# GATv2 layer of 1,250 nodes: the norm between the two layers folded into the next matrices, tile ends issued in steps

## The chip, the core and the metric

The kernel runs on one core of a Trainium2 chip. The core has TensorE (PE, matrix products out of SBUF into PSUM; its weight loads are shown as PEld), VectorE (DVE), ScalarE (ACT), GpSimd (POOL) and SyncE (SP). Each has its own in-order queue, and they meet at semaphores. Data move between HBM and SBUF by DMAs that an engine issues. The metric is the device time of one execution in microseconds (us); lower is better.

## The reference

The inputs are 1,250 nodes with 768 features, 20,000 random edges (sorted by destination), and for each edge one of 34 types. All is float32. Two residual blocks follow one another:

```python
h = relu(layernorm(x))
x = x + gat(h)          # block 1, this case's subject
h = relu(layernorm(x))
x = x + rgcn_gcn(h)     # block 2: 34 relations, then one GCN, on 625-node halves of the indices
```

Block 1 is two GATv2 layers and two norms:

```python
def gatv2(x, Ws, bs, Wd, bd, attn):          # attn: H x D
    fs, fd = x @ Ws + bs, x @ Wd + bd        # N x H x D
    e = leaky_relu(fs[src] + fd[dst], 0.2)
    alpha = segment_softmax(einsum("ehd,hd->eh", e, attn), dst)
    return elu(segment_sum(alpha * fs[src], dst))

h1  = gatv2(h, W1s, b1s, W1d, b1d, attn1)    # 8 heads of 96
h2  = layer_norm(h1 + h) * ln1_w + ln1_b
out = gatv2(h2, Wos, bos, Wod, bod, attno)   # 1 head of 768
out = layer_norm(out) * lno_w + lno_b
```

`ln1_w` and `ln1_b` act per feature, and `h2` is only used as the left operand of the products with `Wos` and `Wod`. A node without an edge gets 0 from the segment sum.

## The kernel before

The kernel is written in a framework that places instructions on engines as the code says, but orders each engine's queue by its own scheduler, from the order of the code and the tiles' dependencies; pools with a number of buffers limit how far ahead a queue runs.

**Front end (0 to 177 us).** `fast_front` ranks the nodes by their number of incoming edges, highest first, by comparing them on TensorE and VectorE; rank and edge slots are scattered to a table in DRAM by GpSimd and read back as `rk` (L949, issued by SyncE), from which `perm`, `permg` and `degf` are copied. The first norm gives `h0` (written to DRAM by SyncE, L791), and its product with `W1s` the source table `fs_d` (L840; here a bias is added by a one-row product of a row of ones with the bias). SyncE also writes zeros and fill values to tables in DRAM (L809 to L815).

**Layer one (177 to 913 us).** The ranked nodes are cut into 10 tiles of 128, one node per partition. Tile k has as many edge slots as its largest degree, `CAPS = (33, 22, 20, 18, 17, 16, 15, 14, 13, 11)`, 179 in all; a tile of more than 20 slots is taken in two chunks, so there are 12 chunks. `attention` (L1189) works through them:

- `start_tile` (L1201) makes a tile's destination rows. In layer one `negated1` (L1407) gathers the tile's `h0` rows, transposes them by TensorE (`to_columns`, L1118; one or both copies out of PSUM by ScalarE, L1125, or the second by VectorE, L1127), multiplies them by `f_w1d` (`dense`, L1131: two halves of 384 columns, six matmuls each) and evicts the negative with the bias to `nfd` (L1414, VectorE).
- `front` (L1213) takes one slot: GpSimd gathers 128 rows of the source table into `fs`, a ring of 24 buffers; VectorE takes z = max(fs, nfd) (L1228), z times attn (L1233) and the sum per head (L1234), the slot's logits. `list_edges(row, n)` (L1388) lets GpSimd send n of the 179 pair scatters that build a later stage's list of edges (`r_pair_d`): 30 at slot 23 of tile 0, then 0.85 per slot, and more at the end.
- `softmax` (L1238) does the exponentials of a chunk; the sums of the two chunks of a tile are brought to one maximum.
- `back` (L1270) scales the slot's row by its weights (ScalarE, 8 instructions, L1286) and adds it into PSUM by a product with the identity, two halves (`ag`, L1288). `back` of a chunk runs beside `front` of the next one.
- `end` (L1302) divides by the softmax's sum (`share`, L1291), applies ELU and calls `finish1` (L1418): add `h0`, norm statistics and scaling (L1423), times `lnw` (L1424), plus `lnb` (L1425), transposes, product with `wos`, plus bias (`fs`, L1431), a product with a quarter of `attn_o` whose row sum is layer two's linear logit term (`wt`, L1433), scatter to the table `fs2_d` by GpSimd, product with `wod`, negative with bias (`fd`, L1440), and a write to DRAM (L1442).

The end of a tile is written whole after its last `back`, and the next-but-one tile's `start_tile` whole in the middle of a chunk. `loads1` (L1399) loads `wos`, `wod` and five rows broadcast to 128 partitions.

**Layer two (913 to 1,395 us)** is `attention` again with one head, `negated2` and `finish2` (L1467). Then come the relations (1,390 to 2,566 us), bound by TensorE, and the GCN.

Of the kernel before, what the change touches and what calls it, by code (L numbers as in the profile page):

```python
# [18 lines left out]
P = 128  # L19
# [607 lines left out]
def fast_front(ctx, tc, f, x, src, dst, edge_type, W1s, b1s, W1d, b1d, attn1, attno, W_rel):  # L627
# [26 lines left out]
    f.consts = ExitStack()  # L654
# [29 lines left out]
    with ExitStack() as front:  # L684
# [33 lines left out]
        ones_row = early.tile([1, P], F32, name="ones_row")  # L718
        nc.vector.memset(ones_row, 1.0)

        def by_heads(a, name):
            n, d = a.shape
            t = const.tile([P, n, d + 1], F32, name=name)
            nc.vector.memset(t[:, :, d], 1.0)
            nc.scalar.dma_start(t[:, :, :d], bass.AP(tensor=a.tensor, offset=a.offset, ap=[[0, P], [d, n], [1, d]]))
            return t

        f.attn_1 = by_heads(attn1, "attn_1")
        f.bias_1 = const.tile([P, D], F32, name="bias_1")
        nc.scalar.dma_start(f.bias_1, bass.AP(tensor=b1d.tensor, offset=b1d.offset, ap=[[0, P], [1, D]]))  # L730
        f.attn_o = by_heads(attno, "attn_o")


# [52 lines left out]
        for j in range(NT):  # L786
            n = min(P, N - j * P)
            row = xs[j]
            sc, sh = norm_scale(nc, small, f, row, n)
            nc.scalar.activation(row[:n], row[:n], AF.Relu, bias=sh[:n], scale=sc[:n])  # L790
            nc.sync.dma_start(f.h0_d[j * P:j * P + n, :], row[:n])  # L791
            to_columns(nc, ps_t, f, hT, j, row, n, both=True)
# [16 lines left out]
        nc.sync.dma_start(f.pair_d.rearrange("(p c) f -> p c f", p=P), fill)  # L809
        zero = prep.tile([P, D], F32, name="zero")  # L810
        nc.vector.memset(zero, 0.0)
        nc.sync.dma_start(f.h2_d[NP:, :], zero)
        for t in range(PT + 1):
            nc.sync.dma_start(f.h1_d[NP + t * P:NP + (t + 1) * P, :], zero)
        nc.sync.dma_start(f.h1_d[f.ZERO:, :], zero[:1])  # L815
# [133 lines left out]
        nc.sync.dma_start(rk, rank_d.rearrange("(k p) f -> p k f", p=P))  # L949
# [195 lines left out]
def fast_rest(ctx, tc, f, x, src, dst, edge_type, W1s, b1s, W1d, b1d, attn1, ln1_w, ln1_b,  # L1145
# [43 lines left out]
    def attention(H, table, negated, attn_e, first, loads, finish, rate, rest, give_back=lambda: None):  # L1189
# [12 lines left out]
        def start_tile(k):  # L1202
            t = Tile()
            t.k, t.S, t.done = k, CAPS[k], []
            t.nfd = rows_tile("nfd", 2)
            nc.vector.memset(t.nfd[:, :, HD], -BIG)
            negated(k, t.nfd[:, :, :HD])
            t.lg = None
            return t

        def front(c, i):

            t, s = c.t, c.first + i  # L1213
            fs = pool.tile([P, RW], F32, name="fs", tag="fs", bufs=ring)
            row = gather(fs[:, :W], table[:, :], f.rec[:, t.k, s, 0:1])
            fs = fs[:, :W].rearrange("p (h e) -> p h e", h=H)
            if t.k == 0 and s == ring - 1:
                list_edges(row, 30)
            elif t.k or s >= ring:
                list_edges(row, rate)  # L1220
            if t.k == NT - 1 and s == t.S - 1:
                list_edges(row, rest)
                f.last_row = row
            if t.lg is None:
                lg = pool.tile([P, S0 * f.H], F32, name="lg", tag="lg", bufs=2)
                t.lg = lg[:, :S0 * H].rearrange("p (s h) -> p s h", h=H)
            z = rows_tile("z", 2)
            nc.vector.tensor_tensor(z, fs, t.nfd, op=ALU.max)  # L1228
            if H == 1:
                nc.vector.scalar_tensor_tensor(z[:, 0, :], z[:, 0, :], 1.0, attn_e[:, 0, :], op0=ALU.mult,  # L1230
                                               op1=ALU.mult, accum_out=t.lg[:, s, :])
            else:
                nc.vector.tensor_mul(z, z, attn_e)  # L1233
                nc.vector.tensor_reduce(t.lg[:, s, :], z, axis=AX.X, op=ALU.add)  # L1234
            c.rows.append(fs)
# [55 lines left out]
        def share(o, ps, by):  # L1291

            if H == 1:
# [8 lines left out]
        def end(t):  # L1302
# [4 lines left out]
            share(o, c.ps, c.den)  # L1307
# [6 lines left out]
            finish(t.k, o)  # L1314
# [9 lines left out]
        tiles = {}  # L1324
# [10 lines left out]
        begin(0)  # L1335
        for i in range(chunks[0].n):
            front(chunks[0], i)
            if i == 3:
                loads()
            if i == chunks[0].n // 2:  # L1340
                begin(1)
        softmax(chunks[0])
        for j, now in enumerate(chunks):
            after = chunks[j + 1] if j + 1 < len(chunks) else None
            for i in range(max(now.n, after.n if after else 0)):
                if i < now.n and after:
                    back(now, i)
                if after and i < after.n:
                    front(after, i)
                if i == now.n // 2:  # L1350
                    begin(j + 2)
            if after:
                softmax(after)
                if j + 2 == len(chunks):
                    for i in range(after.n):
                        back(after, i)
                    give_back()
            if now.first + now.n == now.t.S:
                end(now.t)
# [6 lines left out]
                            f.degf[:, :, None].to_broadcast([P, NT, S0]), op=ALU.is_ge)  # L1366

# [27 lines left out]
    with ExitStack() as one:  # L1395
        bias_1 = f.bias_1
        late = {}

        def loads1():  # L1399
            ap1 = late["pool"] = one.enter_context(tc.tile_pool(name="r_att1", bufs=1, side="right"))  # L1400
            late["wos"], late["wod"] = load_w(ap1, Wos, "wos", "wos"), load_w(ap1, Wod, "wod", "wod")
            for name, a in (("lnw", ln1_w), ("lnb", ln1_b), ("bias_s", bos), ("bias_d", bod), ("attn_o", attno)):
                late[name] = load_row(ap1, a, name)
# [3 lines left out]
        def negated1(k, nfd):  # L1407
# [4 lines left out]
            to_columns(nc, ps_t, f, hT, 0, h0s[k], P, both=True)  # L1412
            ps = dense(nc, ps_t, f, hT, f.w1d, 0, P, tag="mm2")
            nc.vector.scalar_tensor_tensor(  # L1414
                nfd.rearrange("p (a h) d -> p a h d", a=2), ps[:, :, :HW].rearrange("p a (h d) -> p a h d", d=D // H),
                -1.0, bias_1.rearrange("p (a h d) -> p a h d", a=2, d=D // H), op0=ALU.mult, op1=ALU.subtract)

        def finish1(k, o):  # L1418
            lnw, lnb, wos, wod = late["lnw"], late["lnb"], late["wos"], late["wod"]
            bias_s, bias_d, attn_o = late["bias_s"], late["bias_d"], late["attn_o"]  # L1420
# [3 lines left out]
            nc.vector.tensor_mul(o, o, lnw)  # L1424
            nc.vector.tensor_add(o, o, lnb)  # L1425
            hT = pool.tile([P, KC, P], F32, name="hT1", tag="hT1", bufs=1)
            to_columns(nc, ps_t, f, hT, 0, o, P)
            ps = dense(nc, ps_t, f, hT, wos, 0, P, tag="mm2")
            ap1 = late["pool"]
            fs = ap1.tile([P, W2], F32, name="fs2", tag="fs2", bufs=1)  # L1430
            nc.vector.tensor_add(halves(fs, P, f), ps[:, :, :HW], halves(bias_s, P, f))  # L1431
            wt = work.tile([P, D], F32, name="wt2", tag="att_e")
            nc.vector.scalar_tensor_tensor(wt, fs[:, :D], SLOPE / (1.0 - SLOPE), attn_o, op0=ALU.mult, op1=ALU.mult,  # L1433
                                           accum_out=fs[:, D:])
            row = scatter(fs2_d[:, :], fs, f.perm[:, k:k + 1], "fs2")
            if NT - 4 < k < NT - 1:
                list_edges(row, 7 if k < NT - 2 else 40)
            ps = dense(nc, ps_t, f, hT, wod, 0, P, tag="mm2")
            fd = ap1.tile([P, D], F32, name="fd2", tag="fd2", bufs=1)
            nc.vector.scalar_tensor_tensor(halves(fd, P, f), ps[:, :, :HW], -1.0, halves(bias_d, P, f),  # L1440
                                           op0=ALU.mult, op1=ALU.subtract)
            nc.sync.dma_start(nfd2_d[k * P:(k + 1) * P, :], fd)  # L1442

        attention(H, f.fs_d, negated1, f.attn_1, prepare_lists, loads1, finish1, 0.85, 4)


# [11 lines left out]
    def loads2():  # L1458
        for name, a in (("lnw", lno_w), ("lnb", lno_b), ("bias_g", b_gcn)):
            late[name] = load_row(ap2, a, name)  # L1460
        late["ones"] = ap2.tile([1, P], F32, name="ones_r")
        nc.vector.memset(late["ones"], 1.0)
# [4 lines left out]
    def finish2(k, o):  # L1467
        lnw, lnb, bias_g = late["lnw"], late["lnb"], late["bias_g"]
        sc, sh = norm_scale(nc, small, f, o, P)
        row = ap2.tile([P, D], F32, name="x1", tag="x1", bufs=2)  # L1470
# [18 lines left out]
        def root():  # L1489
            ps, _ = dense(nc, ps_t, f, hT, late["wroot"], 0, P, tag="mm2", bias=(late["ones"], late["bias_r"]))  # L1490
# [5 lines left out]
        if k < NT - 3:  # L1496
            root()
        else:
            roots[k] = root

    def negated2(k, nfd):
        nc.sync.dma_start(nfd[:, 0, :], nfd2_d[k * P:(k + 1) * P, :])

    def read_lists():
# [9 lines left out]
        fold = rl.tile([P, P], F32, name="fold")  # L1514
# [10 lines left out]
    attention(1, fs2_d, negated2, f.attn_o, lambda: None, loads2, finish2, 0, 0, give_back)  # L1525
# [129 lines left out]


# [110 lines left out]
```

## Time and profile before

| | |
|---|---|
| time, median of 3 runs | 2768.38 us (2763.95 to 2773.92) |
| the profiled execution | 2772.99 us, span 2771.2 us |
| clock granted to TensorE, mean | 0.93 |
| PE / DVE / POOL / ACT busy | 2355.7 / 1560.9 / 1549.0 / 852.4 us |
| layer one: scalings L1286 on ScalarE | 370.0 us in 1,376 instructions |
| layer one: `ag` products L1288 on PE | 286.9 us in 716 records |
| layer one: L1228, L1233, L1234 on DVE | 169.8, 168.5, 168.0 us |
| layer one: `f_w1d`, `wos`, `wod` products on PE | 83.7, 82.4, 79.3 us, 240 records each |

The rows come from one profiled execution. Busy times are sums over the span, and each stage has another engine ahead, so they are to be read by stretches of time. A group of instructions is named by its line, engine, operation and the tiles it writes and reads; "idle before" is the engine's idle time just ahead of the group, with what ended it. One float32 matmul of the code appears as two records, so 240 records are 120 matmuls.

### The profile page before, as it was taken

How to read it: one execution, taken by the hardware profiler on the slowest of the kernel's cores; microseconds unless marked ns; L12 is line 12 of the kernel's file. 1: busy time of each engine (PE TensorE's matmuls, PEld its weight loads, DVE VectorE, ACT ScalarE, POOL GpSimd, SP SyncE). 2: the span in 40 equal slices, each digit the busy share in tenths (PEclk: the TensorE clock that was granted, in tenths of full speed). 3: DMA queues.
4: the chain of work that ended last, by engine and by line, in shares of the span. 5: the costliest groups of instructions: out<-in, count | busy, mean ns of one | idle time of the engine just before them, and what ended most of it. 6: DMA issues, size and time to landing. Idle time of an engine off the chain costs nothing. (4 is left out here: it accounts for less than half of the span.)

```text
span 2771.2 us, 24164 instructions
## 1 busy us (share of the span) xinstructions
PE 2355.7 (85%) x7759; PEld 1365.4 (49%) x7759; DVE 1560.9 (56%) x2360; ACT 852.4 (31%) x2308; POOL 1549.0 (56%) x1113
## 2 busy tenths in 40 slices
PE   3874484889998467889899999999999999999687
PEld 2431142445545234444456666666666666666254
DVE  7659779999996799999563222222232222210262
ACT  3003592778773122333312112211221212212010
POOL 3137787777872675778375544444444454431471
PEclk7986797999999788999999999999999999999899
DMA  7134453444540775677477777777777777766783
GB/s 248 41 128 146 115 147 95 127 129 131 154 123 29 246 234 170 202 214 216 160 241 194 200 189 187 189 197 197 192 194 187 185 191 197 174 165 152 217 264 117
DMA packets 136419, 476.82 MB, mean 172 GB/s; under 512 B 26323, under 2 KB 28396, under 8 KB 136285
## 3 DMA queue, kind: packets, MB, share of 16 engines
q0 software_dynamic: 83872, 334.60, 46.4%
q1 hardware_dynamic: 47755, 134.03, 13.6%
q10 hardware_dynamic: 4658, 6.57, 0.7%
q8 instruction: 64, 1.05, 0.1%
q14 instruction: 70, 0.57, 0.1%
HBM read 385.90 MB, written 89.32 MB: 171 GB/s over the span
## 5 line engine op out<-in xcount | busy, mean ns | idle before, releaser
L1135 PE MATMUL ps<-wrel,mT 128*128 128x384 f32 x3336 | 1099.1, 486 | 1.1 <-DMA wrel<-in_L_gnn_W_rel_dram 1.1
L1135 PEld LDWEIGHTS ps<-wrel,mT 128*128 128x128 f32 x3336 | 623.0, 190 | 407.1 <-DMA wrel<-in_L_gnn_W_rel_dram 1.0
L1164 POOL DMA_INDIRECT g<-r_h_d,lists x241 | 341.9, 1419 | 516.9 <-DVE g L1565 290.7
L1288 PE MATMUL ag<-fs,identf 128*128 128x384 f32 x716 | 286.9, 532 | 152.4 <-ACT fs L1286 142.0
L1565 DVE TENSOR_TENSOR g<-g,g 128x768 f32<-128x768 f32 x68 | 64.6, 950 | 612.5 <-DMA g<-r_h_d,lists 512.6
L1228 DVE TENSOR_TENSOR z<-fs,nfd 128x776 f32<-128x776 f32 (+1 forms) x358 | 348.5, 990 | 60.0 <-DMA fs<-f_fs_d,rec 37.2
L1286 ACT ACTIVATE fs<-fs,lg 128x96 f32<-128x96 f32 x1376 | 370.0, 363 | 0.3
L1278 PE MATMUL ag<-fs,dg 128*128 128x384 f32 x716 | 251.7, 512 | 81.0 <-ACT dg L1276 81.0
L1168 POOL DMA_INDIRECT r_pair_d<-rec,place x179 | 259.5, 1450 | 59.9 <-issue 46.7
L1164 POOL DMA_INDIRECT fs<-r_fs_d,rec x179 | 244.0, 1363 | 80.7 <-issue 33.4
L1592 POOL DMA_INDIRECT r_h_d<-y,lists x139 | 223.9, 1611 | 110.2 <-ACT y L1591 52.3
L1164 POOL DMA_INDIRECT fs<-f_fs_d,rec x179 | 236.7, 1323 | 77.0 <-issue 50.2
L1288 PEld LDWEIGHTS ag<-fs,identf 128*128 128x128 f32 x716 | 132.4, 200 | 294.0 <-ACT fs L1286 236.5
L1278 PEld LDWEIGHTS ag<-fs,dg 128*128 128x128 f32 x716 | 141.3, 200 | 188.0 <-ACT dg L1276 88.1
L1591 ACT ACTIVATE y<-ps,lists 128x768 f32<-128x768 f32 x71 | 64.0, 901 | 479.8 <-PE ps L1135 479.8
L1591 ACT ACTIVATE y<-ps,rcnt 128x768 f32<-128x768 f32 x68 | 61.3, 901 | 454.6 <-PE ps L1135 454.6
L1230 DVE SCALAR_TENSOR_TENSOR z<-z,attn_o 128x769 f32<-128x769 f32 x179 | 174.4, 993 | 0.0
L1697 DVE TENSOR_TENSOR acc<-acc,nb 128x768 f32<-128x768 f32 x69 | 66.2, 959 | 187.1 <-DMA nb<-r_h_d,srcz 186.3
L1233 DVE TENSOR_TENSOR z<-z,attn 128x776 f32<-128x776 f32 x179 | 168.5, 955 | 0.1
L1234 DVE TENSOR_REDUCE lg<-z 128x8 f32<-128x776 f32 x179 | 168.0, 950 | 0.1
L1627 DVE SCALAR_TENSOR_TENSOR arow<-node,from_f,arow 128x1250 f16<-128x1250 f16 x110 | 166.2, 1511 | 1.7
L1123 PEld LDWEIGHTS pt<-identf,g 128*128 128x128 f32 x834 | 99.8, 141 | 47.5 <-issue 24.5
(282 smaller groups left out, 2322.0 us busy)
## 6 DMA issues: line engine op xcount, KB each, us to landing
wrel<-in_L_gnn_W_rel_dram SPq DMA_DIRECT2D x37, 2304.0 KB
g<-r_h_d,lists POOLq DMA_INDIRECT x241, 4.8
r_nfd_d<-fd SPq DMA_DIRECT2D x10, 384.0 KB
nfd<-r_nfd_d SPq DMA_DIRECT2D x10, 384.0 KB
r_x_d<-xb SPq DMA_DIRECT2D x10, 384.0 KB
x1r<-r_x_d SPq DMA_DIRECT2D x10, 384.0 KB
f_fs_d<-o_s SPq DMA_DIRECT2D x9, 388.0 KB
x<-in_x_dram SPq DMA_DIRECT2D x9, 384.0 KB
```

Source lines behind the costliest of these rows:

```text
L1135: last = nc.tensor.matmul(ps[:n, half, :f.HW], hT[:, k, j * P:j * P + n], w[:, k, cols], start=(k == 0), stop=(k == f.KC - 1 and not bias))
L1164: return nc.gpsimd.indirect_dma_start(out=to, out_offset=None, in_=table, in_offset=bass.IndirectOffsetOnAxis(ap=idx, axis=0))
L1168: s = nc.gpsimd.indirect_dma_start(out=table, out_offset=bass.IndirectOffsetOnAxis(ap=idx, axis=0), in_=rows, in_offset=None, **kw)
L1228: nc.vector.tensor_tensor(z, fs, t.nfd, op=ALU.max)
L1230: nc.vector.scalar_tensor_tensor(z[:, 0, :], z[:, 0, :], 1.0, attn_e[:, 0, :], op0=ALU.mult, op1=ALU.mult, accum_out=t.lg[:, s, :])
L1233: nc.vector.tensor_mul(z, z, attn_e)
L1234: nc.vector.tensor_reduce(t.lg[:, s, :], z, axis=AX.X, op=ALU.add)
L1278: nc.tensor.matmul(c.ps[:, half, :HW], dg, fs[:, 0, half * HW:(half + 1) * HW], start=begin, stop=end)
L1286: nc.scalar.activation(fs[:, h, :HD], fs[:, h, :HD], AF.Copy, scale=t.lg[:, s, h:h + 1])
L1288: nc.tensor.matmul(c.ps[:, half, :HW].rearrange("p (h d) -> p h d", d=HD), f.identf, fs[:, half * H // 2:(half + 1) * H // 2, :HD], start= ...
L1592: s = nc.gpsimd.indirect_dma_start(out=h1_d[:, :], out_offset=bass.IndirectOffsetOnAxis(ap=j.node, axis=0), in_=y, in_offset=None, compute ...
L1627: nc.vector.scalar_tensor_tensor(a, node16, from_f[:, k, s:s + 1], a, op0=ALU.is_equal, op1=ALU.add)
```

## The change

The norm's weight and bias are moved out of the rows and into layer two's matrices: `wos` and `wod` have each row scaled by `ln1_w` (`scaled`, ScalarE), and `ln1_b @ W + b` is made once by one-column products (`bias`). `wod`'s sum is given to its product as a seventh matmul of one row. `wos`'s sum is left out of the table: it is taken into `wod`'s sum for the logits, and added again in layer two's `share` as `bias_s` (the weights of a node's edges sum to one). A node without edges is masked by `has` in layer two's norm. The linear logit term becomes a 769th column of `wos` (`quarters`, DVE), so the product gives it. `bias_1` becomes a one-row matmul as well. So a tile's end has no `lnw`, `lnb`, bias or `wt` pass on VectorE, and ScalarE evicts all three products, half by half.

Products and transposes come as lists of steps of three matmuls or transposes (`product`, `columns`). The loop keeps a list `todo` and issues a share of it at each slot; a tile's `end` is called four slots into the next chunk, and `start_tile` of the next-but-one tile at its first slot. The first list of pairs is 24 instead of 30. `rk` is read by GpSimd. Rows that last into layer two lie in a pool `r_lasting` below the others. The fill and zero writes are ordered after the last write of `h0`. For the last two tiles of layer one the transposed rows lie in buffers of the ring `fs`.

```diff
-        nc.sync.dma_start(rk, rank_d.rearrange("(k p) f -> p k f", p=P))
+        nc.gpsimd.dma_start(rk, rank_d.rearrange("(k p) f -> p k f", p=P))
...
-            negated(k, t.nfd[:, :, :HD])
+            todo.extend(negated(k, t.nfd[:, :, :HD]))
...
-                list_edges(row, 30)
+                list_edges(row, 24)
...
+            if bias is not None:
+                nc.vector.scalar_tensor_tensor(halves(o, P, f), ps[:, :, :HW], by, halves(bias, P, f),
+                                               op0=ALU.mult, op1=ALU.add)
...
+            steps = max(now.n, after.n if after else 0)
+            for i in range(steps if after else 0):
+                if i < now.n:
                     back(now, i)
-                if after and i < after.n:
+                if i < after.n:
                     front(after, i)
-                if i == now.n // 2:
+                if i == 0:
                     begin(j + 2)
+                if i == 3:
+                    while ended:
+                        critical, rest_of = end(ended.pop())
+                        todo.extend(critical + rest_of)
+                for at, what in extra:
+                    if at == (j, i):
+                        todo.extend(what())
+                if i:
+                    run(-(-len(todo) // (steps - i)))
...
             if now.first + now.n == now.t.S:
-                end(now.t)
+                if j + 2 < len(chunks) and len(now.t.done) == 1:
+                    ended.append(now.t)
+                else:
+                    critical, rest_of = end(now.t)
+                    if j + 2 < len(chunks):
+                        todo.extend(critical + rest_of)
+                    else:
+                        for step in critical:
+                            step()
+                        later += rest_of
...
+        def fold(i):
...
+            def bias(half):
...
+                for k in range(KC):
+                    nc.tensor.matmul(ps[:1, half, :HW], cols[:, 1, k:k + 1], w[:, k, at], start=(k == 0), stop=False)
...
+            def scaled(k):
+                nc.scalar.activation(w[:, k, :D], w[:, k, :D], AF.Copy, scale=cols[:, 0, k:k + 1])
...
+            def quarters(k):
+                wt = work.tile([P, D], F32, name="wt2", tag="att_e")
+                nc.vector.scalar_tensor_tensor(wt, wos[:, k, :D], SLOPE / (1.0 - SLOPE), f.attn_o[:, 0, :D],
+                                               op0=ALU.mult, op1=ALU.mult, accum_out=wos[:, k, D:])
...
+        def product(hT, w, width, bias, evict):
...
+                for k in range(3 * part, 3 * part + 3):
+                    nc.tensor.matmul(ps, hT[:, k], w[:, k, at], start=(k == 0), stop=(k == KC - 1 and bias is None))
+                if part:
+                    if bias is not None:
+                        nc.tensor.matmul(ps, f.ones_row, bias[:, at], start=False, stop=True)
+                    evict(ps, half, at)
...
-            nc.vector.scalar_tensor_tensor(
-                nfd.rearrange("p (a h) d -> p a h d", a=2), ps[:, :, :HW].rearrange("p a (h d) -> p a h d", d=D // H),
-                -1.0, bias_1.rearrange("p (a h d) -> p a h d", a=2, d=D // H), op0=ALU.mult, op1=ALU.subtract)
+                nc.scalar.activation(nfd[:, half * H // 2:(half + 1) * H // 2, :], ps.rearrange("p (h d) -> p h d", d=D // H),
+                                     AF.Copy, scale=-1.0)
...
-            nc.vector.tensor_mul(o, o, lnw)
-            nc.vector.tensor_add(o, o, lnb)
...
-            nc.vector.tensor_add(halves(fs, P, f), ps[:, :, :HW], halves(bias_s, P, f))
-            wt = work.tile([P, D], F32, name="wt2", tag="att_e")
-            nc.vector.scalar_tensor_tensor(wt, fs[:, :D], SLOPE / (1.0 - SLOPE), attn_o, op0=ALU.mult, op1=ALU.mult,
-                                           accum_out=fs[:, D:])
...
-            nc.vector.scalar_tensor_tensor(halves(fd, P, f), ps[:, :, :HW], -1.0, halves(bias_d, P, f),
-                                           op0=ALU.mult, op1=ALU.subtract)
...
+                nc.scalar.copy(held["fs"][:, at], ps)
...
+                nc.scalar.activation(held["fd"][:, at], ps, AF.Copy, scale=-1.0)
...
+        for a in (sc, sh):
+            nc.vector.tensor_mul(a, a, f.has[:, k:k + 1])
...
-    attention(1, fs2_d, negated2, f.attn_o, lambda: None, loads2, finish2, 0, 0, give_back)
+    attention(1, fs2_d, negated2, f.attn_o, lambda: None, loads2, finish2, 0, 0, f.bias_s, (), give_back)
```

## The prediction

> **What bounds the kernel now.** I read the page's slices first, for the stage that has slack, then a table of busy time by stretches, then the waits and groups of layer one, and last the timeline of VectorE and GpSimd where the longest wait lies.
>
> ```profile
> PE   3874484889998467889899999999999999999687
> DVE  7659779999996799999563222222232222210262
> POOL 3137787777872675778375544444444454431471
> PEclk7986797999999788999999999999999999999899
> ```
>
> A slice is 69.3 us. Slices 18 to 37 are the relations, where PE is full; the change does not touch them. DVE (VectorE) is at 9 in slices 7 to 12, layer one, and 15 to 19, layer two. So layer one, 177 to 913 us, is where an edit can count.
>
> ```profile
> core 0: us, PE busy (x) PEld busy (x) DVE busy (x) ACT busy (x) POOL busy (x), PEclk, DMA share, GB/s
> 250.00:300.00 50.00, 29.85 (x64) 10.58 (x64) 30.79 (x40) 34.39 (x129) 40.95 (x30) 0.84 0.16 39
> 300.00:400.00 100.00, 63.00 (x157) 27.90 (x158) 90.20 (x136) 73.18 (x264) 81.59 (x60) 0.82 0.48 130
> 400.00:500.00 100.00, 61.51 (x188) 34.68 (x187) 89.79 (x114) 48.03 (x169) 73.13 (x47) 0.81 0.41 115
> 600.00:700.00 100.00, 89.32 (x267) 49.14 (x268) 94.32 (x131) 80.88 (x277) 74.49 (x57) 0.95 0.46 129
> 700.00:800.00 100.00, 92.54 (x285) 50.60 (x284) 94.93 (x134) 72.78 (x248) 82.00 (x59) 0.98 0.51 143
> 866.00:915.00 49.00, 37.23 (x109) 20.82 (x108) 15.03 (x23) 5.68 (x7) 14.10 (x14) 0.93 0.14 44
> ```
>
> Early (300 to 500) DVE has about 90 of 100 us and PE 62: DVE sets the pace, with holes. Late (600 to 800) both DVE and PE have 90 and more: taking work from DVE alone soon meets PE. POOL (GpSimd) is fuller than its column says: each of its 59 instructions of the last whole row has 0.30 us ahead of it, 82 + 18 = 100. In 866 to 915 everything waits.
>
> ```profile
> engine line waited for: us in total, times, longest us
> DVE z L1228 <- DMA fs<-f_fs_d,rec: 37.2, 14, 19.2
> DVE nfd L1414 <- PE ps L1135: 15.4, 4, 8.2
> DVE fd L1440 <- PE ps L1135: 7.2, 3, 6.1
> ```
>
> ```profile
> 285.73 0.97 POOL L1168 DMA_INDIRECT r_pair_d<-rec,place  x1 [0.30 <-issue]
> 287.00 0.99 POOL L1164 DMA_INDIRECT fs<-f_fs_d,rec  x1 [0.30 <-PE ag L1288]
> 291.02 0.97 DVE L1228 TENSOR_TENSOR z<-fs,nfd 128x776 f32<-128x776 f32 x1 [19.21 <-DMA fs<-f_fs_d,rec]
> 402.02 0.96 DVE L1440 SCALAR_TENSOR_TENSOR fd<-ps,bias_d 128x768 f32<-128x768 f32 x1 [6.08 <-PE ps L1135]
> 411.14 0.96 DVE L1414 SCALAR_TENSOR_TENSOR nfd<-ps,bias 128x768 f32<-128x768 f32 x1 [8.16 <-PE ps L1135]
> ```
>
> The first two waits are removable: DVE waits 19.2 us for a gather that stands behind 30 pair scatters in GpSimd's queue, and at the end of tile 0 its queue stands behind products that PE delivers whole.
>
> **The change part by part**
>
> Start. Reading the ranks (`rk`) by GpSimd instead of SyncE: the read follows the last rank scatter on the same queue; it was issued at 106.89 on SyncE, 2.8 us before landing, and SyncE was free since 82.4. The next `o_s` eviction stands behind `dinv` on ScalarE, so a microsecond here is one of the end. No row shows this read from GpSimd: -1 to +1, I take **+0.5**. The zero writes held behind the last `h0_d` write keep SyncE's order: 0.
>
> The list stall. 24 pairs instead of 30: 6 x (0.97 + 0.30) = 7.6, **-7.6**, gather and DVE both that much earlier. The fold of the norm into `wos`/`wod` falls in the same place: 60 short products, 12 scalings, 2 sums. PE was idle 234 to 258 and DVE stands 11.6 us more, so I cost it at 0; without that cover, 60 x 0.33 x 2 = 40 us of PE. It replaces five row broadcasts of 384 KB. Its scale columns come as 1,536 single elements; a 128-row pair scatter of 12-byte rows lands in 3.0 us, so between 3 and, at one packet after another on that row's pace, 12 x 3.0 = 36 us; the cover is 20 us, so 0 to +16, and I take **+1**.
>
> DVE's tile end. L1414, L1424, L1425, L1431, L1433, L1440 leave DVE, 0.95 us each in the groups, 0.875 from start to start: 5.25 us per tile. Six `quarters` come once: +5.25. Tile 0's end also loses its waits 1.43 + 6.08 + 8.16 = 15.7, since products are now issued three matmuls at a time between aggregation slots, a slot or more ahead of who reads them. Early tiles: -15.7 - 4 x 5.25 + 5.25 = -31.5. What is late next is ScalarE, with six evictions per tile in the order of the scalings, and GpSimd: z of slots 24 to 54 follows its gather by only 4 to 10 us, GpSimd needing 2.99 us a slot there to DVE's 3.19. I give back 7: **-24**.
>
> ```profile
> L1286 ACT ACTIVATE fs<-fs,lg 128x96 f32<-128x96 f32 x1376 | 370.0, 363 | 0.3
> L1288 PE MATMUL ag<-fs,identf 128*128 128x384 f32 x716 | 286.9, 532 | 152.4 <-ACT fs L1286 142.0
> L1414 DVE SCALAR_TENSOR_TENSOR nfd<-ps,bias 128x768 f32<-128x768 f32 x10 | 9.5, 952 | 15.6 <-PE ps L1135 15.6
> L1431 DVE TENSOR_TENSOR fs<-ps,bias_s 128x768 f32<-128x768 f32 x10 | 9.5, 950 | 20.5 <-PE ps L1135 20.5
> ```
>
> Late tiles (600 to 866). DVE's period of a 14-slot tile, 49.6 between two shares, would be 44.3. PE has 43.4 of it, and gains four bias products (both halves of `f_w1d` and `wod`). What is one worth? In the source table of the front end a half with its bias row repeats every 4.95 us and one without every 3.95: 1.0, its records 524 ns. [...] Summed, PE's 242 us of the 266 become 242 + 5 x 4.0 = 262: PE is the bound and leaves 4. [...] ScalarE's six evictions a tile, each near the 0.48 of its 128x384 copies, add 2.9 us; it had 73 to 81 of 100, and 6 more fit. GpSimd: slots 96 to 174 took it 268 us with 15 of idle, so it leaves up to 15 plus the lead it has built at slot 174 (27 us). Between -11 and +15 for coupling; I take **-2**.
>
> The tail. T0 = 866.3, the end of the last aggregation; layer two's first z starts at T0 + 47.2. The waits 9.4 and 9.3 of L1431 on the last two products, and 26.9 of the last table scatter, lie here. Gone from the chain: lnw, lnb, bias and quarter passes, 4 x 0.95 = 3.8, twice where tile 8's end stands ahead of tile 9's; but the six pairs now come here: 13 between the last two scatters instead of 7. The table scatter of tile 8 at about T0 + 11.5, 13 x 1.3 = 17, the last scatter at T0 + 30, and from that scatter to z 8.1 as now: T0 + 38, **-9**. Without the pairs behind it, -18; if the evictions wait, 0.
>
> Layer two: two multiplies of 128x1 a tile (0.15 each), the share with bias at its old 0.95: at most 10 x 0.15; **+1.5**. Its DVE is full, so all of it counts. The deferred tile end there uses the same code: 0, bounds -5 to +5.
>
> Sum: 0.5 - 7.6 + 1 - 24 - 2 - 9 + 1.5 = -39.6. With another +6 for what separate sums leave out (each engine that goes faster early meets GpSimd's ring) it is -33. The profiled execution took 2772.99, its span 2771.2; less 33 is 2740. It lies 4.6 above the median shown, 2768.4, so against that: **2735**.
>
> **The rivals**
>
> Full hiding (0.15). ScalarE and PE absorb all of it: -7.6 - 31.5 - 11 - 9 to -18 = -59 to -68 at most, 2700 to 2709. For: late PE waits for ScalarE's scalings 236.5 us on its load side, so steadier feeding could help. Against: PE at 92.5 of 100.
>
> PE and GpSimd take over early too (0.13). Only stall and tail remain: -7.6 - 9 + 2 = -15, 2753. For: z follows its gather so closely, and GpSimd is stretched by DVE. [...] Here a pair scatter takes 0.97 with DVE idle (272 to 287) and 2.32 under z (226 to 252). [...] By the late rows, 1.3 to 1.45 with DVE at 94%, it stays near -33. [...]
>
> ScalarE's queue becomes the wait: slower (0.18). It runs in order; an eviction waiting for PE holds the scalings behind it, these hold the `ag` products, these the ring slots that GpSimd's next gathers need, and then z. Place: eight tiles with six evictions, 48. Against the -49 of the sum before coupling was taken off (-31.5 early and -4 late), it decides at 49/48, about 1 us each. If each costs a slot's scaling, 370.0/172 slots = 2.15: 48 x 2.15 = 103, +54, 2822. For: PE already waits 142 us for ScalarE. Against: the order of instructions puts 17 to 26 scalings between evictions and a product's six matmuls well ahead of them.
>
> No effect (0.05): the scheduler leaves DVE waiting for something else at each place: 2760 to 2776.
>
> **How the numbers follow.** Likeliest, partial hiding, 0.49: 2720 to 2748. With full hiding and the PE case that is 0.77 for faster by over 0.3% (8.3 us, about what a measurement of this kernel can tell from no change), 0.05 within, 0.18 slower. The range 2706 to 2780 leaves out the far end of the slower case and a sliver below.
>
> **What would show it.** Right: DVE's wait before slot 24 near 11.5 us; no DVE wait over 2 us at tile 0's end; `ag` waits on ScalarE no longer than before; shares of the late tiles 47 to 49 apart, PE at 95 or more per 100; last share to layer two's first z near 38. Wrong: DVE waiting on DMA fs throughout (GpSimd), evictions on ScalarE that wait several us for PE, or the first Exp of layer one later than 256 because of the fold.

## The result, and the profile after

The changed kernel takes 2782.97 us (median of 6 runs, 2778.83 to 2784.32) against 2770.70 of the kernel before, run beside it: a ratio of 1.0045, 95% interval 1.0031 to 1.0060. It is slower by 0.45%, where 2735 and a gain were forecast. The profiled spans are 2781.0 and 2771.2 us. The slices of the page after:

```profile
PE   3876684889999577788999999999999999999687
DVE  7659969977884699999663222222222232210262
POOL 3237777766662676787375554444444454431471
PEclk7987997989999798999999999999999999999899
```

```profile
core 0: us, PE busy (x) PEld busy (x) DVE busy (x) ACT busy (x) POOL busy (x), PEclk, DMA share, GB/s
300.00:400.00 100.00, 72.76 (x188) 31.75 (x186) 80.03 (x127) 84.95 (x299) 75.59 (x58) 0.91 0.48 130
600.00:700.00 100.00, 83.86 (x243) 44.66 (x242) 79.89 (x108) 75.16 (x254) 68.81 (x53) 0.90 0.45 126
700.00:800.00 100.00, 89.33 (x271) 50.34 (x270) 88.34 (x130) 83.25 (x278) 71.14 (x57) 0.95 0.49 140
```

From 600 to 700 VectorE fell from 94 to 80 of 100 us, as it should when work is taken from it, but TensorE fell too, from 89 to 84, though it was given more to do. ScalarE and GpSimd are less busy there too (81 to 75 and 74 to 69): the engines wait for one another. Where, the waits between 290 and 900 us say, first TensorE's and then VectorE's:

```profile
engine line waited for: us in total, times, longest us
PE pt L1513 <- DMA h<-f_h_d,f_permg: 36.3, 5, 11.6
DVE att_o L1305 <- PE ag L1294: 25.4, 2, 14.7
DVE hT L1515 <- PE ps L1500: 18.8, 3, 13.2
DVE att_e L1305 <- PE ag L1294: 18.4, 1, 18.4
DVE hT L1515 <- PE pt L1513: 14.4, 2, 9.1
```

The first row had 0.8 us before. TensorE stands at the transposes of a tile's `h0` rows, five times, for their gather. One such place, in the timeline of VectorE, GpSimd and TensorE:

```profile
608.41 0.95 DVE L1535 TENSOR_TENSOR att_o<-att_o,h 128x768 f32<-128x768 f32 x1
617.19 1.99 POOL L1170 DMA_INDIRECT h<-f_h_d,f_permg  x1 [0.30 <-issue]
622.06 1.54 PE L1513 MATMUL pt<-identf,h 128*128 128x128 f32 x6 [9.47 <-DMA h<-f_h_d,f_permg]
623.53 6.36 PE L1500 MATMUL ps<-f_w1d,hT 128*128 128x384 f32 x12
632.05 4.03 PE L1500 MATMUL ps<-f_w1d,hT 128*128 128x384 f32 x12
639.13 0.56 DVE L1515 COPY hT<-pt 128x384 f32<-128x384 f32 x1 [9.09 <-PE pt L1513]
```

Read from the top: the end of an earlier tile adds its `h0` rows (L1535), and with that gives their buffer back. There are three such buffers (`h0r`), and with the end called four slots into the next chunk, and the start at its first, a fourth tile is begun while three still hold theirs. That happens five times: the ends of the two-chunk tiles 0 and 1 are not put off, and from tile 5 on each start meets a late end. So the gather for the fourth can go only after the add. GpSimd does not stand still for it: its queue has four other DMAs between the add and this gather, which starts 9 us after the add and lands some 4.5 us later (the median of these gathers). TensorE has the transposes in its queue well ahead of that, and everything behind them, aggregations too, stands. After the wait its first 12 records of a product take 6.36 us, the next 12 only 4.03. In the last line VectorE has run dry.

Where the time went, from the marks in both traces (first z; share of tiles 0, 4 and 9, the first line of each `end`; first z of layer two; first relation product; end). The last column is the experiment with the end at slot 0, below.

| stretch | before | after, difference | end at slot 0, difference |
|---|---|---|---|
| to the first z | 197.2 | +3.4 | +1.1 |
| to tile 0's share | 167.3 | -11.2 | -12.2 |
| to tile 4's share | 294.2 | +16.5 | -11.9 |
| to tile 9's share | 207.6 | +10.2 | +1.0 |
| to layer two's first z | 47.2 | -7.5 | -10.3 |
| layer two | 482.1 | -0.5 | -4.8 |
| the rest | 1375.6 | -1.1 | +0.4 |
| sum of differences | | +9.8 | -36.7 |

The change itself moves the shares of tiles 2 to 7, since it calls their ends later. The end of each tile's last aggregation is a mark that it does not move. By that mark tile 0 to tile 4 took 294.0 us before, and differs by +16.3 after and -8.8 with the end at slot 0; tile 4 to tile 9 took 211.7, and differs by +9.6 and -3.1. VectorE's own work is not what is late: the first z of tile 9 starts at 809.7 before and at 808.3 after, while that tile's last aggregation ends 19.0 us later.

### The profile page after: what moved, and what is told of

It is laid out like the page before. It is cut to its first block, busy times and chain, and to the rows that moved or that the text cites. A ratio compares the mean times of both kernels' runs of the same rounds, so it can differ in the third digit from the quotient of the medians.

```text
span 2781.0 us, 24438 instructions
## 1 busy us (share of the span) xinstructions
PE 2417.8 (87%) x7903; PEld 1382.8 (50%) x7903; DVE 1515.4 (54%) x2322; ACT 891.5 (32%) x2383; POOL 1517.3 (55%) x1114
## 5 line engine op out<-in xcount | busy, mean ns | idle before, releaser
L1174 POOL DMA_INDIRECT r_pair_d<-rec,place x179 | 230.2, 1286 | 60.5 <-issue 48.1
```

What stands on the lines that cost most here:

```text
L1174: s = nc.gpsimd.indirect_dma_start(out=table, out_offset=bass.IndirectOffsetOnAxis(ap=idx, axis=0), in_=rows, in_offset=None, **kw)
```

## The experiments

Ratios are to the kernel before, run beside each, with 95% intervals. The difference of two kernels is read from their ratios: 0.001 is 2.8 us.

**1. The buffer of the h0 rows.** Four kernels, all from the changed one. The first has four `h0` buffers, at the price of one of the ring's:

```diff
-            h0s[k] = pool.tile([P, D], F32, name="h0", tag="h0r", bufs=3)
+            h0s[k] = pool.tile([P, D], F32, name="h0", tag="h0r", bufs=4)
...
-            fs = pool.tile([P, RW], F32, name="fs", tag="fs", bufs=ring)
+            fs = pool.tile([P, RW], F32, name="fs", tag="fs", bufs=ring - 1)
...
-                hT = pool.tile([P, RW], F32, name="hT1r", tag="fs", bufs=24)[:, :D].rearrange("p (k n) -> p k n", k=KC)
+                hT = pool.tile([P, RW], F32, name="hT1r", tag="fs", bufs=23)[:, :D].rearrange("p (k n) -> p k n", k=KC)
```

> The changed kernel with four buffers for the gathered h0 rows in place of three (and 23 in place of 24 ring buffers, to make room). Theory A, the end called four slots on keeps a third h0 buffer, so the next-but-one tile's gather waits for it and PE, in order, stands at its transposes (36.3 us in five waits, 9.1 and 13.2 us of DVE behind them): those waits go, DVE's waits for hT fall below 5 us in all, shares of late tiles come back to about 50 apart, and the time falls by 20 to 30 us to 2753 to 2763. Rival B, PE is simply full (bias rows, transposes, products): the waits for the gather go but others of PE take their place, and the time stays within 6 us of the change, 2777 to 2785. Rival C, the ring is what limits: one buffer less costs, above 2785.

Measured: 2771.61, ratio 1.0014 (1.0007 to 1.0021), between the ranges of theory A and rival B. The second is its control, with the ring's change alone:

> The changed kernel with 23 ring buffers in place of 24 and nothing else, the control to the run with four h0 buffers. Theory A: the ring is not the limit late (GpSimd leads by 4 to 6 slots only), 2781 to 2787, with the five waits of PE for the gather of h as they were. Rival C: the ring is the limit, over 2790.

Measured: 2809.93, ratio 1.0148 (1.0125 to 1.0171). So the fourth buffer is worth 0.0134, 37 us, and the ring's missing one costs 28, which theory A had not expected. The timeline of the second shows the place:

```profile
270.72 0.95 POOL L1170 DMA_INDIRECT fs<-f_fs_d,rec  x1 [52.20 <-PE ag L1294]
308.96 0.99 POOL L1170 DMA_INDIRECT fs<-f_fs_d,rec  x1 [0.30 <-issue]
312.90 0.97 DVE L1234 TENSOR_TENSOR z<-fs,nfd 128x776 f32<-128x776 f32 x1 [26.79 <-DMA fs<-f_fs_d,rec]
```

The list of 24 pairs hangs on slot 23's gather. With 24 buffers that gather goes at once and the list runs while nothing else is wanted; with 23 it has to wait for the first aggregation (first line), and the list stands in front of the next gathers (second line), for which VectorE waits 26.8 us.

The pair was therefore made again with the list one slot earlier, four buffers and three:

```diff
-            if t.k == 0 and s == ring - 1:
+            if t.k == 0 and s == ring - 2:
                 list_edges(row, 24)
-            elif t.k or s >= ring:
+            elif t.k or s >= ring - 1:
```

> Four h0 buffers and 23 ring buffers, and the first list of pairs one slot earlier, so that it does not stand ahead of a gather that the ring lets go late. Theory A: this second way of freeing the buffer gives what the end at slot 0 gave, and the 27 us that 23 buffers cost were the list's place at slot 23: 2735 to 2750. Rival C, the ring's size costs all along: 2760 to 2772, near the run with the list at slot 23.

> The control of the run with four h0 buffers and the list one slot earlier: the same with three h0 buffers (23 ring buffers, list at slot 22, end four slots on). Theory A or L: as the change, 2778 to 2792, so that the fourth buffer alone is worth the 30 to 45 us. Rival C, the earlier list did it: 2750 to 2760.

Measured: 0.9923 (0.9901 to 0.9946), 2747.47 us, with four; 1.0055 (1.0038 to 1.0073), 2783.90, with three. The control is within 0.0010, 3 us, of the changed kernel, so with the list in its place the ring's buffer costs little, and the fourth `h0` buffer alone gives 0.0132, 37 us. In the first one's trace TensorE's wait for `h` is gone; among TensorE's waits of the control, from 290 to 900 us, it is there:

```profile
PE pt L1513 <- DMA h<-f_h_d,f_permg: 31.5, 5, 12.2
```

**2. The end ahead of the start.** Nothing is added here, only the order is changed, so that the buffer is given back before it is asked for:

```diff
                 if i == 0:
-                    begin(j + 2)
-                if i == 3:
                     while ended:
                         critical, rest_of = end(ended.pop())
                         todo.extend(critical + rest_of)
+                    begin(j + 2)
```

> The changed kernel with the tile's end called at slot 0 of the next chunk, ahead of the next-but-one tile's start, in place of four slots on. Theory A: the buffer is free before the gather is wanted, PE's waits for h fall from 36.3 to under 10 us, the time to 2755 to 2768. Rival B: no more than 6 us of gain. Rival D, the four slots were needed so that the share does not wait for the last aggregation: DVE's wait for ag at each share comes up by 2 to 3 us a tile, and the gain is eaten, 2775 to 2790.

Measured: 2736.93, ratio 0.9884 (0.9861 to 0.9907). That is 0.0161, 45 us, from the changed kernel, more than theory A gave, and it beats both kernels. TensorE's waits for `h` are gone. Its windows and VectorE's waits between 290 and 900 us:

```profile
600.00:700.00 100.00, 97.65 (x297) 53.37 (x295) 86.22 (x119) 78.85 (x262) 82.63 (x58) 0.98 0.47 136
700.00:800.00 100.00, 96.45 (x301) 53.17 (x302) 84.01 (x120) 80.76 (x269) 83.23 (x56) 1.00 0.47 137
...
DVE att_o L1305 <- PE ag L1294: 23.9, 5, 7.3
DVE att_e L1305 <- PE ag L1294: 18.5, 1, 18.5
```

TensorE has 96 to 98 of 100 at a clock of 0.98 to 1.00, and VectorE waits for it at five shares: TensorE is the bound of the late tiles. Rival D came true in part (VectorE waits 2 to 7 us for the last aggregation at these shares), but did not eat the gain.

The order does one thing more than free the buffer: the steps of the start now stand behind the ten steps of the end in `todo`, so that TensorE comes to the transposes of tiles 5 to 9 17 to 31 us after their gather was issued. The fourth buffer, which leaves the steps where they were, shows that the buffer suffices. That it gave 37 us and not 45 can be followed in the traces: it reaches layer two's first z at 876.6 us, earlier than the 881.2 of this kernel, but layer two, which uses the same ring, takes 493.2 us with 23 buffers and 477.3 here. In all five kernels with 23 buffers it takes 487.5 to 493.2 us, in all others 473.2 to 485.1.

**3. Late start, or wait in the queue?** A start moved behind the late end, both at slot 3, also frees the buffer first:

```diff
-                if i == 0:
-                    begin(j + 2)
                 if i == 3:
                     while ended:
                         critical, rest_of = end(ended.pop())
                         todo.extend(critical + rest_of)
+                    begin(j + 2)
```

> The changed kernel with the end still called four slots on, but the next-but-one tile's start moved behind it, to the same slot. It tells the late end from its place relative to the start. Theory A, the buffer of the h0 rows is what matters: PE's waits for h fall from 36.3 to under 10 us, and the time to 2735 to 2750, though the start is three slots later too. Rival D, the late end itself is what costs: 2760 or more, half or less of the 46 us that the end at slot 0 gave.

Measured: 2787.30, ratio 1.0069 (1.0043 to 1.0094). No gain at all, against theory A: of the 36.3 us of waits for `h` 14.5 are left, and the time is no shorter. It raised the question whether any late start costs, buffer or not. Two kernels asked it. One has the end at slot 0 and only the start at slot 3:

```diff
                 if i == 0:
-                    begin(j + 2)
-                if i == 3:
                     while ended:
                         critical, rest_of = end(ended.pop())
                         todo.extend(critical + rest_of)
+                if i == 3:
+                    begin(j + 2)
```

> The kernel with the end at slot 0, with the next-but-one tile's start three slots later (slot 3). Here the buffer of the h0 rows is free when the gather is issued. Theory L, what costs is that the start (gather, transposes, product, eviction of nfd) begins late in the chunk, whether by the buffer or by the code: 2760 to 2790, most of the 46 us lost again. Theory A in its narrow form, PE standing at the head of its queue for a gather: no such wait is made here, 2733 to 2745.

Measured: 2740.89, 0.9901 (0.9870 to 0.9932), with no wait for `h`, within the interval of the start at slot 0. The other is the kernel of the fourth buffer (list at slot 22) with end and start both at slot 3:

> Four h0 buffers, 23 ring buffers, list at slot 22, and both end and start at slot 3. The gather needs no buffer of the tile that ends. Theory L: the late start costs with the buffer free too, 2770 to 2795. Narrow theory A: 2742 to 2755, as with four buffers and the start at slot 0.

Measured: 2764.49, 0.9998 (0.9985 to 1.0011), between the two theories' ranges. So a late start costs nothing by itself when the end is early, and theory L falls there. But end and start together at slot 3 cost 0.0075, 21 us, with the buffer free. There VectorE waits 33.7 us for `ag` at its shares (20.9 with the start at slot 0) and TensorE has 94 of 100, which fits all of a tile's products being crowded into a chunk's last slots; that cause was not tested further. It also fits the first kernel of this section: with both at slot 3 the fourth buffer is worth about 0.0071, 20 us, and the crowding takes as much.

**4. The parts of the change.** All but one are edits of the kernel with the end at slot 0 (0.9884). The list of pairs, 24 against 30 and 18, and 24 in the kernel before:

```diff
-                list_edges(row, 24)
+                list_edges(row, 30)
...
-                list_edges(row, 24)
+                list_edges(row, 18)
...
-                list_edges(row, 30)
+                list_edges(row, 24)
```

> The kernel with the end at slot 0, and 30 pairs again in the first list in place of 24. Theory: DVE's stall before the first gather behind the list is longer by 6 x 1.28 = 7.7 us, of which the tail's six fewer pairs give back 0 to 3: 2741 to 2745. Rival: the stall is covered by PE's late aggregation (the gathers there wait for ring buffers anyway), and the time stays at 2737 plus or minus 2.

> The kernel with the end at slot 0 and 18 pairs in its first list in place of 24. Theory: the gathers behind the list no longer are what VectorE waits for (the six quarters fill, and the wait before slot 24 is one for the exponentials, 6 us), so no more than 2 us come, and the six pairs at the tail cost up to 7.7: 2736 to 2744. Rival: another 7.7 us come as from 30 to 24, 2728 to 2732.

> The kernel before with 24 pairs in its first list in place of 30, nothing else. Theory: DVE's stall of 19.2 us is 6 x 1.28 = 7.7 shorter; the six pairs come back at the tail between two scatters where GpSimd waits 13 us anyway, so 0 to 2 of it is given back: 2761 to 2764 against 2769. Rival: the tile ends behind it are set by PE and give the gain back, 2767 to 2770.

Measured: 0.9924 (0.9898 to 0.9950) with 30, 0.9920 (0.9904 to 0.9937) with 18, and 0.9958 (0.9946 to 0.9971) for the kernel before with 24. That last one is the forecast stall by itself; its place in VectorE's timeline:

```profile
282.74 0.97 DVE L1228 TENSOR_TENSOR z<-fs,nfd 128x776 f32<-128x776 f32 x1 [11.67 <-DMA fs<-f_fs_d,rec]
```

19.2 us became 11.67, 7.5 less; 7.7 was worked out. In that trace layer two's first z starts 5.5 us earlier; the rest of its 11.7 us of time lies behind it, in code that is the same. In the kernel with the end at slot 0, VectorE waits 6.3 us there again with 30, and the share of tile 9 starts at 850.3 instead of 844.3 us; but the six fewer pairs at the tail give it back, and layer two's first z starts at 881.1 and 881.2. So the 11 us by which the ratio with 30 is worse are not placed by the trace. With 24 there is no wait for this gather, so 18 can give nothing there, and six more pairs at the tail lengthen the wait for layer two's first rows from 24.2 to 31.7 us; with 10 us by the ratio it costs more than theory gave. Fewer is better only down to the length that the cover has.

Products issued whole, instead of spread over the slots:

```diff
-                    run(-(-len(todo) // (steps - i)))
+                    run(99)
```

> The kernel with the end at slot 0, but every list of steps issued at once, not spread over the slots. Theory: spreading was meant to keep aggregations coming between the pieces; without it the waits of DVE for PE at tile ends return, 3 to 6 us a tile over seven tiles: 2755 to 2780. Rival: PE is in order and full either way, and the order of its work moves the time by less than 8 us, 2729 to 2745.

Measured: 2793.33, 1.0088 (1.0071 to 1.0106), 57 us slower than with spreading, where 18 to 43 were expected. VectorE's waits between 290 and 900 us, and GpSimd's, name another victim than the tile ends:

```profile
DVE z L1234 <- DMA fs<-f_fs_d,rec: 66.1, 34, 4.8
POOL fs L1170 <- PE ag L1294: 54.1, 29, 8.2
```

Whole products hold up the aggregations, these the ring's buffers, and so the gathers: GpSimd waits 54.1 us for aggregations against 15.1 with spreading, and VectorE 66.1 us for gathers against 6.3. So the 57 us that spreading is worth come through the ring.

The one-row bias products left out:

```diff
-            return columns(hT, h0s[k], True) + product(hT, f.w1d, D, f.bias_1, evict)
+            return columns(hT, h0s[k], True) + product(hT, f.w1d, D, None, evict)
...
-            return columns(hT, o, False) + product(hT, wos, W2, None, to_table), product(hT, wod, D, late["bias_d"], negative)
+            return columns(hT, o, False) + product(hT, wos, W2, None, to_table), product(hT, wod, D, None, negative)
```

> The kernel with the end at slot 0, without the one-row bias products of f_w1d and wod (four a tile, so the two biases are left out of the computation). Theory P, PE is the bound of the late tiles (93 to 98 busy of 100 from 500 to 800 us): six late tiles x 4 x 0.9 = 22 us of PE go, 12 to 22 us of time, 2715 to 2725. Rival: ScalarE's evictions or VectorE end the waits there, and less than 6 us come, 2731 or more.

Measured: 2726.14, 0.9839 (0.9823 to 0.9856), 12.6 us less, at the foot of what theory P gave. The row of these products among the groups of 177 to 925 us in the changed kernel:

```profile
L1503 PE MATMUL ps<-bias,ones_row 1*128 1x384 f32 x40 | 18.2, 533 | 0.0
```

40 records are 20 one-row products, one for each half of `f_w1d` in the ten tiles: 18.2 us, 0.91 each. The late windows then have TensorE at 94.6 and VectorE at 88 to 91: the bound is nearly shared.

The share of tile 1's first chunk held back on VectorE:

```diff
-            share(o, c.ps, c.den, bias)
+            first_share = share(o, c.ps, c.den, bias)
...
-                share(e, t.done[0].ps, c.old)
+                with tc.issue_after(first_share.ins):
+                    share(e, t.done[0].ps, c.old)
```

> The kernel with the end at slot 0, and the share of tile 1's first chunk ordered behind the share of its second on VectorE. VectorE's wait of 18.5 us for ag at that share is in every version of the change. Theory: VectorE goes on with z meanwhile, the wait goes, and since VectorE is the bound from 400 to 500 (92 busy of 100), 10 to 18 us come: 2719 to 2728. Rival: PE is what ends that stretch, the wait moves to the next thing that reads PE's products (nfd), and the time stays within 4 us of 2737.

Measured: 2741.50, 0.9896 (0.9880 to 0.9913): no gain, as the rival said. The two waits in VectorE's timeline, first with the end at slot 0:

```profile
401.88 0.96 DVE L1305 TENSOR_TENSOR att_e<-ag,old 128x768 f32<-128x768 f32 x1 [18.45 <-PE ag L1294]
```

Then with the share held back:

```profile
408.00 1.84 DVE L1234 TENSOR_TENSOR z<-fs,nfd 128x776 f32<-128x776 f32 x2 [22.39 <-ACT nfd L1528]
```

The wait only changes its name: with the end at slot 0 TensorE is busy without a gap from 383 to 402 us (19.0 of 19.0) with tile 0's end and tile 2's start, and whatever reads its next result waits.

**5. The rank table by SyncE again**, in the changed kernel:

```diff
-        nc.gpsimd.dma_start(rk, rank_d.rearrange("(k p) f -> p k f", p=P))
+        nc.sync.dma_start(rk, rank_d.rearrange("(k p) f -> p k f", p=P))
```

> The changed kernel with the rank table read by SyncE again. The front end ended 3.4 us later after the change, 2.3 of it by the landing of this read (111.97 against 109.68). Theory: GpSimd's read costs about 1.1 of it, since DVE was 1.2 late already at 74 us: 2781 to 2782.5. Rival: all 3.4 are its doing, 2779.5. If the front end is the same here, the 3.4 are not from the read.

Measured: 2777.81, 1.0039 (1.0022 to 1.0055): below what either theory gave, but not to be told from the changed kernel. The copy out of the table starts at 111.3 us here, and between 109.7 and 112.8 in the kernels that read it by GpSimd: the 3.4 us to the first z are mostly scatter of the front end between executions.

## Why the prediction was wrong

The sign was wrong by one step. It is the sentence on the tile's end, "What is late next is ScalarE, with six evictions per tile in the order of the scalings, and GpSimd", for which 7 us were given back. TensorE's own wait for the gather of `h0` rows stands in no term of the sum: it was put at nothing without a reason. The step moved the start to a chunk's first slot and the end four slots on, and the start issues that gather, which was not followed to its buffer: three for four live tiles. It was forecast -24 early and -2 late; the changed kernel shows +16.5 and +10.2, with 36.3 us of that wait, and a fourth buffer alone is worth 37 us; the order, which does more than free the buffer, gives 45. The name of the pool and its `bufs=3` could be read in the code.

With the buffer free the terms can be compared one by one, by the last column of the table:

- The list stall: -7.6 worked out; -7.5 of wait in the kernel before with 24 pairs, 5.5 us up to layer two, and 11.7 us of its whole time (8.0 to 14.9 by the interval). The size was right. What was taken to be left of it (11.5 us) did not stay: with the end at slot 0 VectorE waits 6.0 us earlier instead, for the fold (below), and the gather leaves 7.8 us sooner after the first z than in the kernel before with 24 pairs; why GpSimd gets through the list sooner stays open. The six `quarters` did not fill it, they start at 288 us, behind this place. The stretch to tile 0's share gave 12.2.
- Early tiles: -24; measured -11.9, half (-8.8 by the last aggregations). The step that failed is "also loses its waits 1.43 + 6.08 + 8.16 = 15.7". They were not the price of products delivered whole, but of TensorE having more to do in an 11-slot chunk than time. In their place stands one wait of 18.5 us (17.0 with products issued whole), and holding back its reader only renamed it.
- Late tiles: -2; measured +1.0 (-3.1 by the last aggregations). The size was right, and so was the reason: TensorE at 96 to 98 of 100. But "PE has 43.4 of it" was read too low: the trace before has TensorE busy for 46.0 us of that 14-slot tile's 49.6 (and for 244.6, not 242, of the 266), and with the 4.0 of the bias rows the tile is full. So its shares stay 49.6 apart, and not 47 to 49. Bias rows were taken at 1.0 us from the row of the front end; measured 0.91 for one row. The -11 that bounds the -2 on one side, and that full hiding adds up too, is shown by no run: the late tiles measured +1.0, and leaving out all four bias rows a tile made the whole kernel 12.6 us shorter.
- The tail: -9, 38 us from the last share; measured 36.9, and 39.7 in the changed kernel. Right.
- Layer two: +1.5; measured -4.8, or -0.5 in the changed kernel. Its loop has the new order of end and start too. Most of the 4 us is not clear of scatter: the two executions of layer two's old code took 482.1 and 478.7 us, and six kernels with both at slot 0, the end first, 473.2 to 481.2.
- The fold at 0: one sign of being wrong came true here, "the first Exp of layer one later than 256 because of the fold".

The lines of that Exp, before and then after, with what stands ahead of it in ScalarE's queue and who waits for it:

```profile
256.70 0.31 ACT L1252 ACTIVATE lg<-lg 128x128 f32<-128x128 f32 x1 [26.10 <-DVE lg L1251]
262.56 2.58 ACT L1472 ACTIVATE wod<-wod,ln_cols 128x768 f32<-128x768 f32 x3 [9.18 <-PE b_ps L1464]
266.45 0.31 ACT L1258 ACTIVATE lg<-lg 128x128 f32<-128x128 f32 x1
266.79 0.38 DVE L1260 TENSOR_REDUCE den<-lg 128x8 f32<-128x128 f32 x1 [6.81 <-ACT lg L1258]
```

TensorE's one-column products wait 14.6 us for `ln_cols`, in a stretch where it was idle before; ScalarE's scalings of `wod` wait 9.2 us for these products, and the Exp stands behind the scalings. VectorE waits 6.8 us for it (6.0 with the end at slot 0), where it had no such wait before. It falls just ahead of where the list stall was, and what it costs by itself was not separated.

The sum forecast was -33, and the span with the end at slot 0 is 36.7 shorter. That they are so near is in part luck: a smaller gain early stands against larger ones at the stall and in layer two, and against the 6 held back for coupling.

Of the rivals, the slower one had the right form, an in-order queue that holds aggregations, ring and z, but the wrong queue: ScalarE's evictions do wait for TensorE, 24.4 us for `nfd` and 13.9 for `fd` between 290 and 900 in the changed kernel, but 28.5 and 33.0 in the faster one with the end at slot 0. They wait where TensorE is the bound anyway. Nor did GpSimd take over: VectorE's waits for gathers in that stretch fell from 37.2 us to 21.7, and to 6.3 with the end at slot 0.

## What to carry to other kernels

When a software pipeline is shifted, count the live copies of each buffer that the shifted stages hold, DMA destinations first: a later release and an earlier claim can need one buffer more, and an in-order engine that reads the DMA turns the lack into a stall of everything behind it, here 36.3 us of TensorE in five waits. Before paying for another buffer, try the release ahead of the claim, and both early: at slot 0 that gained 45 us here, at slot 3 nothing. And a wait on an engine that is full can come back under another name when its readers are reordered: here 18.45 us on TensorE as 22.39.

## What the runs showed of the hardware

TensorE's waits for `h` cost more than their length in the changed kernel, and the granted clock is lower with them. The five are of 11.6, 9.5, 4.6, 6.6 and 4.0 us; the first 12 records of the `f_w1d` product behind each take 6.45, 6.36, 5.49, 4.76 and 5.39 us, the next 12 of it 4.03 to 4.08. The clock is 0.61, 0.62, 0.65, 0.74 and 0.79 in the 8 us behind them, and 1.00 in the 10 to 12 us after that. The windows around the wait of 9.5 us, the one shown above:

```profile
606.00:612.00 6.00, 4.88 (x11) 1.78 (x12) 6.00 (x9) 5.98 (x23) 4.91 (x4) 1.00 0.53 141
612.00:622.00 10.00, 0.59 (x2) 0.00 (x0) 10.00 (x16) 1.22 (x2) 8.33 (x6) 0.62 0.54 154
622.00:630.00 8.00, 7.94 (x19) 4.62 (x20) 6.02 (x7) 5.60 (x17) 6.09 (x4) 0.62 0.37 99
630.00:640.00 10.00, 10.00 (x34) 5.54 (x34) 0.91 (x3) 8.78 (x31) 1.91 (x2) 1.00 0.16 41
```

It is 1.00 before the wait and 0.62 in the 10 us of it, as in the first 8 us of work after it, in which 12 records take 6.36 us and not 4.03. 6.36 is 1.58 times 4.03, and 1.00 is 1.61 times 0.62. So 9.5 us of wait cost about 2.3 more in this product alone. That is in line with the gain of 45 us where 36.3 us of wait were taken away, and of 37 where 31.5 were, though how much of the difference it makes was not separated.
